# An adjacency-masked two-layer graph kernel: the first mirror's mask moved ahead of strip 4, and half of graph 0's x1 transposed by TensorE

## The chip, the cores and the metric

The kernel runs on one core of a Trainium2 chip. Its time is the device time of one execution in microseconds (us). Engines are named as in the profile: PE is TensorE, DVE is VectorE, ACT is ScalarE, POOL is GpSimd, SP is SyncE, which here only issues transfers (DMAs).

## The reference

There are 16 graphs of 1024 nodes with 256 features each. `adj` holds 0 and 1 and is symmetric. Cut to what matters:

```python
# layer 0
h = x
e0 = leaky(einsum('bid,bjd->bij', h * a0[:, 0], h))    # leaky slope 0.2
alpha = sigmoid(where(adj == 1, e0, -big))
x = layernorm(x + einsum('bij,bjd->bid', alpha, h) + bias)
# layer 1
H = x @ W
s, d = H @ a_src, H @ a_dst
e = where(adj != 0, exp(-leaky_relu(s[:, :, None] + d[:, None, :], 0.2)), 0)
h_prime = einsum('bnm,bmo->bno', e, H) / rowsum(e)
x = layernorm(x + elu(h_prime))
```

The reference has further cases for `adj` values 2 to 4. The kernel has a second, general pass for them, which runs only if a flag says that such values occur; with these inputs it doesn't.

## The kernel before

`one_kind_pass` works through the graphs in one order that is written out by hand: inside it the framework does not reorder, so each engine runs its instructions as the Python code emits them, and waits where an operand or a buffer is not ready. Everything is float32, but for `adj`, which is bfloat16. A graph's 1024 nodes are eight tiles of 128 rows; 256 features are two chunks of 128. "x1" is the output of layer 0.

Each graph b goes through three stages.

*Strips.* The scores are symmetric, so only the upper triangle is computed. `strip(b, jt)` (L194 to L218) makes rows jt*128 onward of the triangle: PE multiplies (`pe`, L208) in chunks of up to 512 columns, ACT takes two hyperbolic tangents of each chunk (L216 into `tb`, L217 into `low`), DVE takes the larger (L218). `tb` has four buffers, `low` two, the PSUM tile `pe` three. `finish` (L220) multiplies by the adjacency into `al` on DVE (L224) and lets POOL add the diagonal (L234). The lower triangle is the mirror of the upper one. For graphs 1 and up it goes through DRAM: `dump(b, t)` turns 32x32 blocks of strip t on DVE (L240) and writes them with four SP transfers (L244), and `gather(b, t)` (L248) reads them back in one SP transfer as column t of the rows below. The gathered values still lack the adjacency; `mask(b, t)` (L252 to L255) multiplies it in on DVE, in one instruction for rows 1 to 3 and one for rows 4 to 7 where t is 0. Column tile 0 of `al` is thus complete only after `mask(b, 0)`.

Beside the strips of graph b, layer 1 of graph b-1 is prepared: `project(b-1, t)` (L354) multiplies tile t of the transposed x1 (`x1T`) by W on PE (`pH`, L368), and three ACT instructions take the result to `H` and `pq` (L376 to L378). The list `projects` says after which strip which tiles are projected. `share_p` (L390) then transposes a column of `pq` on PE (`prow`, L394), copies it on ACT, and sends it through DRAM to all partitions with two POOL transfers (L398, L400).

*sum0.* `sum0(b, t)` multiplies column tile t of `al` with x: eight matmuls on PE over the row tiles (L315; the profile has two records for each matmul). `t` counts up, so the first one needs column tile 0. DVE adds the bias and takes the statistics, POOL computes the norm, and ACT applies it (`scale0`, L304). In the same stage DVE runs masks 3 to 6 and the weights of layer 1 of graph b-1 (L412).

*sum1.* Layer 1's sum for graph b-1 (L419, again on PE), with the elu, the residual and the second norm.

How x1 is transposed: `save_x1(b, g)` (L337) stores half g (four row tiles) of x1 in DRAM with one SP transfer, `fetch_x1(b, g)` (L345) reads it back with eight SP transfers so that 32x32 blocks stand in transposed places, and `turn_x1(b, g)` (L350) turns each block on DVE (L352). For graphs 1 to 14 all this lies in the sum0 and sum1 stages. For graph 0 there is no sum1 stage ahead of graph 1's strips, so its second half is saved, fetched and turned during graph 1's strips, and its tiles 4 to 7 are projected after strip 7.

The start (graph 0) makes its mirror with PE transposes (`mirror`, L257, L263) and its transposed x likewise (`transpose_x`, L182, L189); `ident` is the identity they use, `ps_t` a PSUM pool of two tiles.

Of the kernel before, what the change touches and what calls it, by code (L numbers as in the profile page):

```python
# [9 lines left out]
F32 = mybir.dt.float32  # L10
# [8 lines left out]
P = 128  # L19
HALF = 512  # L20
# [9 lines left out]
def one_kind_pass(  # L30
# [31 lines left out]
    nc = tc.nc  # L62
    B, N, D = x.shape
    NT = N // P
    ND = D // P
    HT = HALF // P
# [10 lines left out]
    ps_t = ctx.enter_context(tc.tile_pool(name="ps_t", bufs=2, space=PSUM))  # L77
# [22 lines left out]
    def adj_rows(b, j0, j1, columns):  # L100

        for g in range(2):
            k0, k1 = max(j0, g * HT), min(j1, (g + 1) * HT)
            if k0 < k1:
                yield slice(k0, k1), adjs[b, g][:, k0 - g * HT : k1 - g * HT, columns]

    def load_blocks(dst, src, n0, n):


        v = src[ds(n0, n), :].rearrange("(nb nn) (c q dd) -> q c nn nb dd", nn=SQ, c=ND, dd=SQ)  # L110
        for c in range(ND):
            for q in range(P // SQ):
                nc.sync.dma_start(
                    dst[ts(q, SQ), c, ds(n0, n)].rearrange("p (nb dd) -> p nb dd", dd=SQ), v[q, c]
                )
# [19 lines left out]
    ident = const.tile([P, P], F32, tag="ident", name="ident")  # L135
# [58 lines left out]
    def strip(b, jt):  # L194


        if jt == 0:
            als[b] = one.tile([P, NT, N], F32, tag="al", name=f"al_{b}")
        width = N - jt * P
        tb = four.tile([P, N], F32, tag="tb", name=f"tb_{b}_{jt}")  # L200
        tbs[b, jt] = tb
        n_chunks = -(-width // HALF)
        per = -(-(width // P) // n_chunks) * P
        for n, o in enumerate(range(0, width, per)):
            w = min(per, width - o)
            pe = ps_e.tile([P, HALF], F32, tag="e", name=f"pe_{b}_{jt}_{n}")
            for c in range(ND):
                nc.tensor.matmul(  # L208
                    pe[:, 0:w],
                    lhsT=xTs[b][:, c, ts(jt, P)],  # L210
                    rhs=xas[b][:, c, ds(jt * P + o, w)],
                    start=(c == 0),
                    stop=(c == ND - 1),
                )
            low = two.tile([P, HALF], F32, tag="low", name=f"low_{b}_{jt}_{n}")
            nc.scalar.activation(tb[:, ds(o, w)], pe[:, 0:w], AF.Tanh, scale=0.5)  # L216
            nc.scalar.activation(low[:, 0:w], pe[:, 0:w], AF.Tanh, scale=0.5 * SLOPE)  # L217
            nc.vector.tensor_tensor(tb[:, ds(o, w)], tb[:, ds(o, w)], low[:, 0:w], ALU.max)  # L218
# [27 lines left out]
    def gather(b, t):  # L246

        nc.sync.dma_start(  # L248
            als[b][:, t + 1 :, ts(t, P)], mirs[b, t].rearrange("(jt p) i -> p jt i", p=P)
        )  # L250

    def mask(b, t):  # L252
        for js, rows in adj_rows(b, t + 1, NT, ts(t, P)):
            v = als[b][:, js, ts(t, P)]
            nc.vector.scalar_tensor_tensor(v, v, 1.0, rows, ALU.add, ALU.mult)  # L255
# [50 lines left out]
    x1s, mv0s, r0s = {}, {}, {}  # L306
# [22 lines left out]
    def scale0(b, t):  # L329
        scale(x1s[b][:, t, :], *r0s[b][t])  # L330


    x1Ts, Hs, pqs, p_bcs, es = {}, {}, {}, {}, {}
# [3 lines left out]
    def save_x1(b, g):  # L337

        if g == 0:
            x1_rows[b] = dram.tile([N, D], F32, tag="x1_rows", name=f"x1_rows_{b}")  # L340
        nc.sync.dma_start(
            x1_rows[b].rearrange("(t p) d -> p t d", p=P)[:, ts(g, HT), :], x1s[b][:, ts(g, HT), :]
        )

    def fetch_x1(b, g):  # L345
        if g == 0:
            x1Ts[b] = one.tile([P, ND, N], F32, tag="x1T", name=f"x1T_{b}")
        load_blocks(x1Ts[b], x1_rows[b], g * HALF, HALF)

    def turn_x1(b, g):  # L350
        v = x1Ts[b][:, :, ts(g, HALF)]
        nc.vector.transpose(v, v)  # L352

    def project(b, t):  # L354

        if t == 0:
            if b < B - 1:
                H = one.tile([P, NT, D + 1], F32, tag="H", name=f"H_{b}")
                Hs[b] = [H[:, m, :] for m in range(NT)]
            else:  # L360
                Hs[b] = []
                for g in range(2):
                    H = two.tile([P, HT, D + 1], F32, tag=f"adj{g}", name=f"H_{b}_{g}")
                    Hs[b] += [H[:, m, :] for m in range(HT)]
            pqs[b] = small.tile([P, NT, 2], F32, tag="pq", name=f"pq_{b}")
        pt = ps_acc.tile([P, D + 2], F32, tag="acc", name=f"pH_{b}_{t}")
        for c in range(ND):
            nc.tensor.matmul(  # L368
                pt,
                lhsT=x1Ts[b][:, c, ts(t, P)],  # L370
                rhs=Wx[:, c, :],
                start=(c == 0),
                stop=(c == ND - 1),
            )
        w = Hs[b][t][:, D : D + 1]
        nc.scalar.activation(w, pt[:, 1:2], AF.Exp, scale=-SLOPE)  # L376
        nc.scalar.activation(pqs[b][:, t, :], pt[:, 0:2], AF.Exp, scale=SLOPE - 1.0)
        nc.scalar.mul(Hs[b][t][:, 0:D], pt[:, 2:], w)  # L378
# [117 lines left out]
    for b in range(1, B):  # L496
        prev, done = b - 1, b - 2
        last = b == B - 1

        projects = [[0, 1], [2], [3], [4, 5], [6], [7], [], []]  # L500
        if prev == 0:

            projects = [[], [0], [1], [2], [3], [], [], [4, 5, 6, 7]]
            turn_x1(0, 0)
        for jt in range(NT):
            strip(b, jt)
            if prev == 0 and jt == 0:
                for t in range(HT, NT):
                    scale0(0, t)
                save_x1(0, 1)  # L510
            finish(b, jt)
            if jt < NT - 1:
                dump(b, jt)
            if prev == 0 and jt == 1:
                fetch_x1(0, 1)
            if prev == 0 and jt == 6:
                turn_x1(0, 1)
            if jt >= 1:
                gather(b, jt - 1)
            for t in projects[jt]:  # L520
                project(prev, t)
            if jt == (6 if prev > 0 else 7):
                share_p(prev)
            if jt >= 5:
                mask(b, jt - 5)
        check_pq(prev)
        if not last:
            load_x(b + 1)
            new_xT(b + 1)
            load_blocks(xTs[b + 1], x[b + 1], 0, N)  # L530

        for t in range(NT):
            if 1 <= t < 5:
                mask(b, t + 2)
            for m in ([], [], [0, 1], [2], [3], [4], [5], [6, 7])[t]:
                weights(prev, m)
            if done >= 0:
                scale1(done, t)
                if t in (3, 7):
                    store(done, t - 3, HT)  # L540
            sum0(b, t)
            if t == 5 and not last:
                load_adj(b + 1, 0)
            if t in (5, 6):
                scale0(b, 2 * t - 10)
                scale0(b, 2 * t - 9)
            if t == 6:
                save_x1(b, 0)
            if t >= NT - CHECKS:
                check_adj(b, t - NT + CHECKS)  # L550
        if not last:
            load_adj(b + 1, 1)


        for t in range(NT):
            acc = acc1(prev, t, ps_acc, "acc")
            for m in range(NT):
                sum1(prev, t, acc, m)
            if last and t == 6:
                turn_x1(b, 1)  # L560
            if last and t == 7:
                weights(b, 0)
            elu(prev, t, acc)
            if last and t == 7:
                weights(b, 1)
            if t >= 1:
                add(prev, t - 1)
            if t == 0:
                fetch_x1(b, 0)
            if t in (1, 2):  # L570
                scale0(b, 2 * t + 2)
                scale0(b, 2 * t + 3)
            if t == 2:
                save_x1(b, 1)
            if t == 4:
                fetch_x1(b, 1)
                turn_x1(b, 0)
            if not last and t in (3, 5):
                turn_x(b + 1, (t - 3) // 2)
            if not last and t == 6:  # L580
                turn_x1(b, 1)
            if last and t in (5, 6):
                for n in range(HT):
                    project(b, (t - 5) * HT + n)
                spread_p(b, t - 5)
        if not last:
            add(prev, NT - 1)
            r1s[prev] = center(mv1s[prev], f"1_{prev}")
# [53 lines left out]
    t = NT - 1  # L642
# [394 lines left out]
```

## Time and profile before

| what | value |
|---|---|
| runs | 1302.4, 1303.8, 1304.43 us; median 1303.8 |
| profiled execution | 1304.77 us, span 1303.0 us, granted PE clock 0.992 |
| PE, sum0 (L315) | 2048 records, 449.3 us busy, 380 ns each |
| PE, sum1 (L419) | 2048 records, 448.9 us busy |
| PE, strips (L208) | 768 records, 267.3 us busy |
| PE, projections (L368) | 512 records, 129.4 us busy |
| DVE, mask (L255) | 150 instructions, 76.5 us busy, 257 to 979 ns |
| gathers (L248) | 105 transfers, 1.7 to 4.7 us from issue to landing |
| first gather of a graph | 448 KB, median 4.1 us to landing |
| x1 store and fetch | 512 KB, 4.3 us; 64 KB each, 2.5 us |

Times are those of one profiled execution. The span is the time from its first to its last instruction; the run's own time has 1.8 us more. A matmul's record lasts about 380 ns though the next starts some 218 ns later: matmuls overlap, so the step between records is what counts. "Idle before" in a row is the time that the engine stood still just ahead of these instructions, with what released it.

### The profile page before, as it was taken

What the parts mean: (1) busy time and instruction counts of PE and PEld (TensorE: products, weight loads), DVE (VectorE), ACT (ScalarE), POOL (GpSimd) and SP (SyncE); (2) the same over time, 40 slices, a digit from 0 to 9 for tenths busy, and PEclk for the clock granted to TensorE, in tenths of its full rate; (3) what the DMA queues carried; (4) which work ended last, traced back from release to release, by engine and by line L of the source; (5) the groups of instructions that cost most, each with busy time, mean ns of one, the idle gap of its engine ahead of it and who ended that gap; (6) DMA issues with size and microseconds to landing.
All of it is one profiled execution on the core that took longest, in us unless ns stands there. A gap on an engine that the chain in (4) does not pass through costs nothing.

```text
span 1303.0 us, 17447 instructions
## 1 busy us (share of the span) xinstructions
PE 1265.0 (97%) x5445; PEld 1022.0 (78%) x5445; DVE 925.4 (71%) x2000; ACT 650.7 (50%) x1459; POOL 295.3 (23%) x606
## 2 busy tenths in 40 slices
PE   7979999999999999999999999999999999999995
PEld 5758788787877878788787887878778787887884
DVE  5665876868868586786868868587785868768664
ACT  4543544645545564545645545564545735446424
POOL 2212121321212222121221212223121221213203
PEclk9989999999999999999999999999999999999998
DMA  9386487694857948487594956948578594876211
GB/s 215 65 180 118 86 189 140 128 202 84 187 112 170 181 95 193 88 188 155 116 203 82 192 120 155 185 95 198 89 175 172 107 194 83 190 139 129 82 17 68
DMA packets 609173, 181.30 MB, mean 139 GB/s; under 512 B 486200, under 2 KB 591664, under 8 KB 609072
## 3 DMA queue, kind: packets, MB, share of 16 engines
q1 hardware_dynamic: 588480, 138.61, 49.0%
q0 software_dynamic: 20592, 41.48, 18.0%
q8 instruction: 46, 0.75, 0.2%
q14 instruction: 55, 0.45, 0.1%
HBM read 152.44 MB, written 61.14 MB: 164 GB/s over the span
## 4 chain that ended last, share of the span: by engine, by line
PE 82%; issue 5%; SPq 4%; DVE 4%; DMA 3%; POOL 1%; ACT 1%; POOLq 0%; DVEq 0%
PE acc L315 34%; PE acc L419 30%; PE pe L208 13%; PE pH L368 4%; SPq L244 3%; DMA mir<-tb 2%; DVE al L224 1%; DVE tb L240 1%; DVE tb L218 1%; ACT tb L216 1%; DVE al L255 1%; POOL r L285 1%; ACT low L217 0%; DMA x<-in_x 0%; SPq L248 0%
## 5 line engine op out<-in xcount | busy, mean ns | idle before, releaser
L315 PE MATMUL acc<-x,al 128*128 128x256 f32 x2048 | 449.3, 380 | 5.3 <-DVE al L255 5.3
L419 PE MATMUL acc<-H,e 128*128 128x257 f32 x2048 | 448.9, 380 | 0.6 <-DVE e L412 0.6
L315 PEld LDWEIGHTS acc<-x,al 128*128 128x128 f32 x2048 | 386.4, 190 | 62.8 <-DVE al L255 10.9
L419 PEld LDWEIGHTS acc<-H,e 128*128 128x128 f32 x2048 | 387.7, 190 | 58.4 <-DVE e L412 1.3
L208 PE MATMUL pe<-xa,xT 128*128 128x384 f32 (+3 forms) x768 | 267.3, 486 | 0.0
L208 PEld LDWEIGHTS pe<-xa,xT 128*128 128x128 f32 x768 | 141.5, 189 | 86.9 <-issue 46.0
L304 ACT ACTIVATE x<-x,mr,r 128x256 f32<-128x256 f32 x128 | 69.2, 592 | 231.6 <-POOL mr L300 199.9
L412 DVE SCALAR_TENSOR_TENSOR e<-p,pq,adj 128x1024 f32<-128x1024 f32 x128 | 159.8, 1270 | 20.8 <-DMA p<-p_row 17.8
L283 POOL TENSOR_SCALAR ve<-mv 128x4 f32<-128x4 f32 (+3 forms) x51 | 17.9, 350 | 676.5 <-DVE mv L277 671.2
L441 ACT ACTIVATE h<-acc,rinv 128x256 f32<-128x256 f32 x127 | 59.7, 470 | 192.7 <-DVE rinv L436 176.5
L216 ACT ACTIVATE tb<-pe 128x512 f32<-128x512 f32 (+1 forms) x192 | 94.3, 491 | 117.2 <-PE pe L208 78.5
L218 DVE TENSOR_TENSOR tb<-tb,low 128x512 f32<-128x512 f32 (+1 forms) x192 | 103.9, 546 | 60.2 <-ACT low L217 48.9
L368 PE MATMUL pH<-Wx,x1T 128*128 128x258 f32 x512 | 129.4, 387 | 8.5 <-issue 8.4
L435 DVE TENSOR_SCALAR rinv<-acc 128x1 f32<-128x1 f32 x128 | 20.1, 157 | 162.2 <-PE acc L419 162.1
L368 PEld LDWEIGHTS pH<-Wx,x1T 128*128 128x128 f32 x512 | 99.1, 194 | 45.5 <-issue 22.9
L121 ACT ACTIVATE junk<-adj,minus 128x2048 bf16<-128x2048 bf16 x64 | 127.3, 1989 | 0.0
L234 POOL TENSOR_TENSOR al<-ident,al 128x128 f32<-128x128 f32 x128 | 68.2, 533 | 241.2 <-DVE al L224 241.0
L224 DVE SCALAR_TENSOR_TENSOR al<-tb,adj 128x512 f32<-128x512 f32 (+7 forms) x132 | 97.5, 738 | 5.0
L323 DVE SCALAR_TENSOR_TENSOR x<-acc,bias_bc 128x256 f32<-128x256 f32 x128 | 54.0, 422 | 61.9 <-PE acc L315 61.9
L217 ACT ACTIVATE low<-pe 128x512 f32<-128x512 f32 (+1 forms) x192 | 93.0, 485 | 0.0
L255 DVE SCALAR_TENSOR_TENSOR al<-al,adj 128x512 f32<-128x512 f32 (+3 forms) x150 | 76.5, 534 | 1.9 <-DMA al<-mir 1.9
L240 DVE STREAM_TRANSPOSE tb<-tb 128x896 f32<-128x896 f32 (+6 forms) x105 | 74.8, 712 | 3.6
(63 smaller groups left out, 903.7 us busy)
## 6 DMA issues: line engine op xcount, KB each, us to landing
adj<-in_adjT POOLq DMA_DIRECT2D x30, 1024.0 KB, 9.2
x_rows<-x SPq DMA_DIRECT2D x32, 512.0 KB, 4.3
x1T<-x_rows SPq DMA_DIRECT2D x256, 64.0 KB, 2.5
x<-in_x SPq DMA_DIRECT2D x15, 1024.0 KB, 5.9
xT<-in_x SPq DMA_DIRECT2D x120, 128.0 KB, 3.4
out<-y SPq DMA_DIRECT2D x30, 512.0 KB, 5.3
p<-p_row POOLq DMA_DIRECT2D x15, 512.0 KB, 4.3
mir<-tb SPq DMA_DIRECT2D x60, 112.0 KB, 2.4
```

The lines of the kernel that those rows point to most:

```text
L121: nc.scalar.activation(junk, rows, AF.Square, bias=minus1, scale=2.0, accum_out=chk[:, b * CHECKS + n : b * CHECKS + n + 1],)
L208: nc.tensor.matmul(pe[:, 0:w], lhsT=xTs[b][:, c, ts(jt, P)], rhs=xas[b][:, c, ds(jt * P + o, w)], start=(c == 0), stop=(c == ND - 1),)
L216: nc.scalar.activation(tb[:, ds(o, w)], pe[:, 0:w], AF.Tanh, scale=0.5)
L217: nc.scalar.activation(low[:, 0:w], pe[:, 0:w], AF.Tanh, scale=0.5 * SLOPE)
L218: nc.vector.tensor_tensor(tb[:, ds(o, w)], tb[:, ds(o, w)], low[:, 0:w], ALU.max)
L224: nc.vector.scalar_tensor_tensor(als[b][:, jt, c0:c1], tbs[b, jt][:, c0 - jt * P : c1 - jt * P], 1.0, adjs[b, jt // HT][:, jt % HT, c0:c1] ...
L240: nc.vector.transpose(tb, tb)
L255: nc.vector.scalar_tensor_tensor(v, v, 1.0, rows, ALU.add, ALU.mult)
L315: nc.tensor.matmul(acc, lhsT=als[b][:, jt, ts(t, P)], rhs=xs[b][:, jt, :], start=(jt == 0), stop=(jt == NT - 1),)
L368: nc.tensor.matmul(pt, lhsT=x1Ts[b][:, c, ts(t, P)], rhs=Wx[:, c, :], start=(c == 0), stop=(c == ND - 1),)
L412: nc.vector.scalar_tensor_tensor(es[b][:, m, :], p_bcs[b], pqs[b][:, m, 1:2], adjs[b, m // HT][:, m % HT, :], ALU.mult, ALU.min)
L419: nc.tensor.matmul(acc, lhsT=es[b][:, m, ts(t, P)], rhs=Hs[b][m], start=(m == 0), stop=(m == NT - 1),)
```

## The change

Two things change, both in `one_kind_pass`. First, `mask(b, 0)` of every graph from 1 on is emitted before `strip(b, 4)`, where it stood after strip 5's other work; masks 1 and 2 stay after strips 6 and 7. Second, for graph 0 alone, `save_x1`, `fetch_x1` and `turn_x1` of the second half go, and a new function `transpose_x1` after strip 2 makes the same half of `x1T` with eight PE transposes into two PSUM tiles and one ACT copy of each. With it, graph 0's projections 4 to 7 move from after strip 7 to after strips 4, 5 and 6, and its `share_p` from after strip 7 to after strip 6, as for the other graphs.

```diff
+    def transpose_x1(b):
+
+        for c in range(ND):
+            pt = ps_t.tile([P, HT, P], F32, tag="t", name=f"px1T_{b}_{c}")
+            for t in range(HT):
+                nc.tensor.transpose(pt[:, t, :], x1s[b][:, HT + t, ts(c, P)], ident)
+            nc.scalar.copy(x1Ts[b][:, c, ts(1, HALF)], pt.rearrange("p t q -> p (t q)"))
...
         projects = [[0, 1], [2], [3], [4, 5], [6], [7], [], []]
         if prev == 0:
 
-            projects = [[], [0], [1], [2], [3], [], [], [4, 5, 6, 7]]
+            projects = [[], [0], [1], [2], [3, 4], [5, 6], [7], []]
             turn_x1(0, 0)
         for jt in range(NT):
+            if jt == 4:
+                mask(b, 0)
             strip(b, jt)
             if prev == 0 and jt == 0:
                 for t in range(HT, NT):
                     scale0(0, t)
-                save_x1(0, 1)
             finish(b, jt)
             if jt < NT - 1:
                 dump(b, jt)
-            if prev == 0 and jt == 1:
-                fetch_x1(0, 1)
-            if prev == 0 and jt == 6:
-                turn_x1(0, 1)
+            if prev == 0 and jt == 2:
+                transpose_x1(0)
             if jt >= 1:
                 gather(b, jt - 1)
             for t in projects[jt]:
                 project(prev, t)
-            if jt == (6 if prev > 0 else 7):
+            if jt == 6:
                 share_p(prev)
-            if jt >= 5:
+            if jt >= 6:
                 mask(b, jt - 5)
```

## The prediction

> **What bounds the kernel now.** I read the page first, for the engine that fills the span, then stretches of equal work side by side, then the chain of waits and the timeline where they differ.
>
> ```profile
> span 1303.0 us, 17447 instructions
> PE 1265.0 (97%) x5445; PEld 1022.0 (78%) x5445; DVE 925.4 (71%) x2000; ACT 650.7 (50%) x1459; POOL 295.3 (23%) x606
> L315 PE MATMUL acc<-x,al 128*128 128x256 f32 x2048 | 449.3, 380 | 5.3 <-DVE al L255 5.3
> ```
>
> TensorE (PE) is the bound: only its idle or slow stretches are to be won. The last row gives one such place: the matmuls of sum0 (L315) wait 5.3 us in all for the mask (L255). The list of waits says 14 times, at most 0.4 us each. Graphs are numbered by b; 14 is graphs 2 to 15. Next the three first strip stages (graphs 1, 2, 3), each from the first strip to where sum0 runs on, by the view of windows:
>
> ```profile
> core 0: us, PE busy (x) PEld busy (x) DVE busy (x) ACT busy (x) POOL busy (x), PEclk, DMA share, GB/s
> 57.30:92.03 34.73, 25.96 (x82) 16.74 (x81) 23.58 (x39) 17.18 (x53) 7.22 (x16) 0.85 0.69 137
> 147.56:171.11 23.55, 23.17 (x85) 15.06 (x83) 19.07 (x34) 16.19 (x49) 7.37 (x14) 1.00 0.54 106
> 226.25:249.79 23.54, 23.17 (x85) 15.06 (x83) 19.07 (x34) 16.19 (x49) 7.37 (x14) 1.00 0.53 102
> ```
>
> Graph 1 needs 11 us more than the others, at a granted clock of 0.85. The chain of waits (start, us, what) shows where:
>
> ```profile
> 74.01 2.61 PE pe L208 x12
> 76.62 8.43 issue
> 85.05 6.55 PE pH L368 x16
> 91.92 0.28 PE prow L394
> 92.19 7.83 PE acc L315 x36
> ```
>
> PE is through with its strips at 76.62, idles 8.43 us, and then runs the last four projections (16 records of pH) at 0.41 us each; in graph 2, eight records take 1.74 us, 0.218 each. So there is a hole and a slow clock after it. The timeline of graph 1 says what the projections waited for:
>
> ```profile
> 64.98 0.38 SPq L341 DMA_DIRECT2D x_rows<-x  x1
> 65.45 6.07 SPq L244 DMA_DIRECT2D mir<-tb  x8
> 71.57 4.31 SPq L113 DMA_DIRECT2D x1T<-x_rows  x8
> 75.98 0.43 SPq L248 DMA_DIRECT2D al<-mir  x1
> 83.75 1.20 DVE L352 STREAM_TRANSPOSE x1T<-x1T 128x1024 f32<-128x1024 f32 x1
> ```
>
> The second half of x1 goes out (64.98), comes back in eight transfers on SP (71.57), and is turned by VectorE (DVE) at 83.75, behind strip 6 in DVE's order. The fetch also holds back the first gather to 75.98. Last, the end of graph 2's strip stage, by the timeline:
>
> ```profile
> 161.85 0.44 SPq L248 DMA_DIRECT2D al<-mir  x1
> 164.43 0.71 DVE L240 STREAM_TRANSPOSE tb<-tb 128x512 f32<-128x512 f32 x1
> 167.00 0.69 DVE L218 TENSOR_TENSOR tb<-tb,low 128x512 f32<-128x512 f32 x1 [1.86 <-DMA mir<-tb]
> 170.13 0.60 PE L315 MATMUL acc<-x,al 128*128 128x256 f32 x2
> 170.50 1.15 DVE L255 SCALAR_TENSOR_TENSOR al<-al,adj 128x384 f32<-128x384 f32 x2
> 171.11 2.21 PE L315 MATMUL acc<-x,al 128*128 128x256 f32 x9 [0.38 <-DVE al L255]
> ```
>
> sum0 starts at 170.13, does its first row tile (two records), and waits for the first piece of mask 0. DVE has that mask only at 170.50, after strip 5, though it sat idle for 1.86 us ahead of strip 4's L218. Was the data there? For L248 in the window 161:163 the trace answers:
>
> ```profile
> DMA to landing us min/median/max: 4.1/4.1/4.1
> ```
>
> So gather 0 lands at 161.85 + 4.1 = 165.95, inside that idle time.
>
> **What the Trainium skill says.** "TensorE: Matmul & The Clock Gate", Part 1: after an idle window of about 3.4 us the array falls to half rate and warms up again under load. The trace agrees: 0.41 against 0.218 us after 8.43 us idle. The same page, Part 4 (PE-mode transpose): a full 128x128 transpose through PSUM takes about 275 ns in context. Here L263's take 272 to 300 ns and seven of them fill 0.93 us, a step of 0.11. "Perfetto Trace Analysis", Tensor Engine Instruction: DVE and ScalarE (ACT) are strict FIFOs, so a mask waiting for its gather holds strip 4 behind it; the trace always shows one DVE order. "DMA: Bandwidth & Descriptors", Anatomy of one DMA: a transfer has some 2 us fixed, mostly the receipt. The store and fetch that go pay that twice; here they land in 4.3 and 2.5 us (medians).
>
> **The change, part by part.**
>
> Graph 1, removed: one store and eight fetches on SP, one turn on DVE (1.2 us), and with them the hole (8.43) and the slow clock: 16 x (0.41 - 0.218) = 3.1. Together 11.5 us of PE time.
>
> Graph 1, added: eight transposes after strip 2, 8 x 0.11 = 0.9 us on PE, all on the path. Their input is scaled by ACT before 65.0; PE gets there at about 67.5, so no wait. Two ACT copies of 128x512 from PSUM at 0.586 each (L388's row by form), with a step of some 0.5 as L216 and L217 have: about 1.0 us on ACT behind strip 2's tanh, from about 68.8. Before, ACT had caught up by 69.7 (first idle 0.39); with the copies it does by 70.7, about where PE brings strip 3's first chunk. PSUM buffers of strips 3 and 4 need ACT's work on chunks three earlier, done by 68.8. So the copies are hidden; uncovered they would cost 1.0 to 1.2.
>
> Graph 1, moved: projections go to steps 4, 5 and 6, the same instructions (per tile four PE records and three short ACT ones). Project 7 now stands just ahead of share_p's transpose, which waits for ACT's pq: before it waited 0.33 there in the same order, at warm clock I take 0.47 (0.38 for the last record, 0.02, 0.24 for ACT, 0.05, less the step of 0.22). share_p moves from step 7 to 6: its two POOL transfers pass POOL's diagonal of strip 7, as in all later graphs, and that diagonal is needed only by the last tile of sum0, over 20 us later. SP's first gather moves from 75.98 to about 71.6, when the dumps are out.
>
> Graph 1's sum: a stage without stall takes 170.13 - 147.56 = 22.57; plus 0.9, plus 0.47, plus 0.15 that strip 2 already waits for ACT (2.74 against 2.59 in the chain) = 24.1. Before: 34.73. Gain 10.6 us, with sum0 at about 81.4.
>
> Is DVE in time there? It is packed from 65.95 on. It ends strip 3 at 74.56; gather 0, issued at 71.6, lands at 75.7. So mask 0 stalls DVE 1.1 us and ends at 76.8; strips 4, 5, 6 take 1.92 + 1.55 + 1.14, and mask 1's first piece 0.39: done at 81.8. sum0's second tile needs it at 81.4 + 3.48 + 0.87 = 85.8. Slack 4 us.
>
> Graphs 2 to 15, mask 0 ahead of strip 4: two DVE instructions, 1.08 us of DVE's time (170.50 to the next start at 171.58), no DMA. Moved past: L218, L224, L240 of strips 4 and 5. Behind the waiting mask stand strip 4's max (which frees a `low` buffer for ACT), its product (then POOL's diagonal), its turn (then SP's dump 4). Start 165.95, end 167.03 against 167.00 when strip 4's data comes: nothing. In graph 3 the gather takes 4.3 us and the same sum gives 0.3 us delay of strips 4 and 5, which nobody waits for: sum0 reads those rows' own parts from its fifth tile on, and ACT needs the `low` buffer only at 170.06. What goes: PE's stall at 171.11. The records step by 0.218 (27.46 us for 126), so the third could start at 170.13 + 0.436 = 170.57; the stall is 0.54. Next late would be mask 1: after strip 6, whose tanh ends at 170.44, it runs from about 171.7, first piece done at 172.1, needed at 170.13 + 4.35 = 174.5. Slack again. Both-sided bound for one graph: 0.38 (the idle that the row shows, from a modelled end) to 0.54; a loss only in the case below. I take 14 x 0.54 = 7.6. Later stages (weights, sum1, turns) take their time from PE and shift with it.
>
> Sum against the profiled execution, 1304.77 us by the clock of the runs (span 1303.0 and 1.8 around it): 1304.8 - 10.6 - 7.6 = 1286.6. The median of the runs, 1303.8, lies 1 us lower: 1285.6. I say 1286.
>
> **Rivals.** (A) Only graph 1 gains, because something else is late for sum0 in graphs 2 to 15 at the same moment: 1303.8 - 10.6 = 1293. For it: DVE is the second engine. Against: the slacks above, and the wait list names only the mask. (B) Graph 1 gains less: ACT's copies bare (1.2), the transposes at the cold step of 0.22 that L189 shows at the start of the run (0.9 more), a stall of about 1 us on a PSUM buffer: 3 us, 1289. For it: ACT and DVE are behind PE in that stage already. (C) Slower: mask 0 does not go by gather 0 alone. The chain of waits puts a later dump ("DMA mir<-tb", ending at 170.52) ahead of the mask. If the mask can start only at W, DVE stops there, and mask 1, 4.61 us of strips behind, comes late too: PE's stall is W - 168.4 (W + 1.08 + 4.61 + 0.39 against 174.48). With W = 170.52 that is 2.1 us in place of 0.54, in 14 graphs and about the same loss in graph 1: +24 - 10.6 = +13, 1317. It decides from W - 168.4 = 0.54 + 10.6/14, W = 169.7, a landing 7.8 us after the issue. Against: the longest landing of any gather is 4.7 us, and in graph 6 the chain reaches the same mask (485.24) through DVE alone at the same distance from PE. (D) The change doesn't do what it says, the wait merely moving to another release in all stages: within 0.2%.
>
> **How the numbers follow.** Forecast 0.76, B 0.11, A 0.08, C 0.04, D 0.01. The forecast's own ends: 5.3 to 7.6 for the 14 graphs, 9.5 to 11.1 for graph 1, and 1 us of scatter: 1284 to 1290. With B inside and part of A's way, 1283.5 to 1291. Faster by over 0.2% (2.6 us, about what a measurement of this kernel can tell) 0.95, same 0.01, slower 0.04.
>
> **What would show it.** Right: no issue gap in graph 1's chain, its stage near 24 us at a clock near 1.0; no L315 wait for L255 in the list; mask 0 some 4 us after its gather's issue; graph to graph 78.14 us in place of 78.68. Wrong: L218 of strip 4 released by L255 over 2 us late, a new PE wait on mask 1 or on `pe` buffers, or pH records still at 0.4 us.

## The result and the profile after

The changed kernel takes 1285.04 us (median of 4 runs, 1284.06 to 1285.33) against 1303.57 us for the kernel before: a ratio of 0.9856, with a 95% interval of 0.9845 to 0.9868. The gain is 18.5 us by the medians. The two profiled executions lie further apart (spans 1303.0 and 1282.3 us, 20.7), because the one of before, 1304.77 us, is slower than its other runs and the one of after, 1284.06 us, the fastest of its own. All times that follow from traces are differences of these two executions.

From the page after: the span, the share of the engines, and the row of sum0's matmuls, whose idle time before them was 5.3 us.

```profile
span 1282.3 us, 17435 instructions
PE 1258.7 (98%) x5453; PEld 1021.8 (80%) x5453; DVE 923.6 (72%) x1999; ACT 651.9 (51%) x1461; POOL 294.5 (23%) x606
L315 PE MATMUL acc<-x,al 128*128 128x256 f32 x2048 | 445.5, 379 | 0.0
```

The list of waits has no matmul of sum0 any more. The new function moved later lines by 7 or 8: projections are now L376, sum1 is L427, the transpose of share_p is L402.

The view of windows (stretch, its length, busy time of each engine, granted clock, DMA share, GB/s) of the kernel after: graph 1's strip stage, graph 2's, and graph 2's sum0.

```profile
56.86:80.80 23.94, 23.62 (x90) 15.62 (x89) 19.74 (x31) 18.26 (x54) 5.78 (x15) 1.00 0.66 126
136.27:158.84 22.57, 22.57 (x82) 14.86 (x81) 18.87 (x33) 15.76 (x48) 6.90 (x13) 1.00 0.52 100
158.84:186.47 27.63, 27.63 (x130) 24.33 (x129) 22.41 (x47) 12.71 (x23) 8.12 (x14) 1.00 0.90 196
```

And graph 2's sum0 in the kernel before, in the same view:

```profile
170.13:198.41 28.28, 27.90 (x131) 24.25 (x130) 23.29 (x48) 12.71 (x23) 7.64 (x14) 1.00 0.89 185
```

Graph 1's strip stage falls from 34.73 to 23.94 us, a gain of 10.79, and its clock is back from 0.85 to 1.00. Each later sum0 falls from 28.28 to 27.63, a gain of 0.64 or 0.65; in graphs 2 to 15 this makes 9.0. In sum0, PE's busy time now equals the length of the stretch. The change is thus worth 19.8 us by the stages. The other 0.9 of the 20.7 us lies ahead of graph 1's strips and behind graph 15's sum0, where the two kernels do the same. It is scatter: in a second trace of the changed kernel graph 1 starts at 57.98 and not at 56.86.

The chain of waits of the kernel after (start, us, what), at graph 1's transposes, at the end of its strips, and at graph 2's sum0:

```profile
64.34 2.58 PE pe L208 x8
66.92 0.87 PE px1T L359 x8
67.79 0.87 PE pH L376 x4
...
79.05 0.89 PE pH L376 x4
79.93 0.02 issue
79.95 0.17 ACT H L384
80.13 0.07 ACT pq L385
80.20 0.04 issue
80.24 0.28 PE prow L402
...
159.01 27.63 PE acc L315 x128
```

Eight transposes take 0.87 us; the projections run at 0.22 us a record; the hole is gone. What is left is the short wait for ACT ahead of share_p's transpose: of the 23.94 us, graph 2's 22.57 and the transposes' 0.87 leave 0.50 for it. In graph 2 all 128 records of sum0 now follow one another, where before the chain broke after two.

The timeline of the kernel after, graph 1 first, then graph 2:

```profile
67.71 1.08 ACT L360 COPY x1T<-px1T 128x512 f32<-128x512 f32 x2
69.99 0.49 ACT L216 ACTIVATE tb<-pe 128x384 f32<-128x384 f32 x1 [0.61 <-PE pe L208]
70.67 0.44 SPq L248 DMA_DIRECT2D al<-mir  x1
74.14 1.16 DVE L255 SCALAR_TENSOR_TENSOR al<-al,adj 128x384 f32<-128x384 f32 x2 [0.56 <-DMA al<-mir]
...
150.56 0.44 SPq L248 DMA_DIRECT2D al<-mir  x1
154.97 1.16 DVE L255 SCALAR_TENSOR_TENSOR al<-al,adj 128x384 f32<-128x384 f32 x2 [1.11 <-DMA al<-mir]
156.04 0.68 DVE L218 TENSOR_TENSOR tb<-tb,low 128x512 f32<-128x512 f32 x1
158.84 6.42 PE L315 MATMUL acc<-x,al 128*128 128x256 f32 x29
```

ACT makes the two copies and still waits 0.61 us for PE at strip 3, so they are hidden. In graph 2 the mask starts 4.4 us after its gather's issue, at once when the data is there, and strip 4's max (L218) comes at 156.04, 0.4 us after ACT has its data ready. Counted from the start of its stage, this max is 0 to 1.5 us later than before in graphs 2 to 15; PE sees none of it.

### The profile page after: what moved, and what is told of

Read it like the earlier page. It is cut to its first block, busy times and chain, and to the rows that moved or that the text cites. A ratio compares the mean times of both kernels' runs of the same rounds, so it can differ in the third digit from the quotient of the medians.

```text
span 1282.3 us, 17435 instructions
## 1 busy us (share of the span) xinstructions
PE 1258.7 (98%) x5453; PEld 1021.8 (80%) x5453; DVE 923.6 (72%) x1999; ACT 651.9 (51%) x1461; POOL 294.5 (23%) x606
## 4 chain that ended last, share of the span: by engine, by line
PE 93%; issue 4%; POOL 1%; DVE 0%; DMA 0%; ACT 0%; SPq 0%; POOLq 0%
PE acc L315 34%; PE acc L427 30%; PE pe L208 19%; PE pH L376 8%; POOL r L285 1%; DMA x<-in_x 0%; PE pxT L189 0%; PE pal L263 0%; POOL ve L283 0%; DVE e L420 0%; PE prow L402 0%; POOL mr L300 0%; POOL n L288 0%; POOL n L289 0%; POOL n L290 0%
## 5 line engine op out<-in xcount | busy, mean ns | idle before, releaser
L427 PE MATMUL acc<-H,e 128*128 128x257 f32 x2048 | 448.8, 380 | 0.6 <-DVE e L420 0.6
L427 PEld LDWEIGHTS acc<-H,e 128*128 128x128 f32 x2048 | 387.7, 189 | 58.5 <-DVE e L420 1.3
L218 DVE TENSOR_TENSOR tb<-tb,low 128x512 f32<-128x512 f32 (+1 forms) x192 | 103.6, 545 | 32.5 <-ACT low L217 32.1
L376 PE MATMUL pH<-Wx,x1T 128*128 128x258 f32 x512 | 126.6, 381 | 0.0
L376 PEld LDWEIGHTS pH<-Wx,x1T 128*128 128x128 f32 x512 | 97.2, 190 | 36.0 <-issue 14.3
L217 ACT ACTIVATE low<-pe 128x512 f32<-128x512 f32 (+1 forms) x192 | 93.0, 485 | 0.0
L255 DVE SCALAR_TENSOR_TENSOR al<-al,adj 128x512 f32<-128x512 f32 (+3 forms) x150 | 76.4, 534 | 20.6 <-DMA al<-mir 20.6
```

The source lines that it names most:

```text
L376: nc.tensor.matmul(pt, lhsT=x1Ts[b][:, c, ts(t, P)], rhs=Wx[:, c, :], start=(c == 0), stop=(c == ND - 1),)
L427: nc.tensor.matmul(acc, lhsT=es[b][:, m, ts(t, P)], rhs=Hs[b][m], start=(m == 0), stop=(m == NT - 1),)
```

## The experiments

The theory: two gains that don't depend on each other, both PE time. In graph 1 it is the hole with the slow clock behind it, in graphs 2 to 15 the wait for mask 0. DVE's own waits cost nothing as long as mask 1 comes in time for sum0's second tile. The rivals are named with each run. All ratios are against the kernel before on the same chip, with 95% intervals; differences to the changed kernel are judged by the traces.

**The mask alone.** The kernel before, with:

```diff
         for jt in range(NT):
+            if jt == 4:
+                mask(b, 0)
             strip(b, jt)
...
-            if jt >= 5:
+            if jt >= 6:
                 mask(b, jt - 5)
```

> The kernel before with the move of mask 0 alone. Theory (two gains that don't depend on each other: PE's wait for mask 0 in graphs 2 to 15, and the hole in graph 1): graphs 2 to 15 lose 0.65 us each, 9.0 in all, as in the changed kernel. In graph 1 the first gather still goes out behind the fetch and lands near 79.8, so the mask holds strips 4 to 6 and the turn of x1 behind it on DVE: the turn starts near 85.5 instead of 83.75, and the hole grows by 1.8. Sum 1303.6 - 9.0 + 1.8 = 1296.4. Rival (the move is worth something only with the rest of DVE's work made lighter; alone the waiting mask costs what it saves): 1302 to 1305.

Measured: 1297.25 us, ratio 0.9949 (0.9935 to 0.9962). In the trace every sum0 of graphs 2 to 15 takes 27.63 us, as in the changed kernel, so the mask's 0.65 us a graph need nothing else. In graph 1 the hole grew, by the chain of waits of this kernel:

```profile
77.76 9.51 issue
87.27 6.78 PE pH L368 x16
```

9.51 against 8.43 us: DVE waited 5.1 us for the late gather, and the turn of x1 stood behind it. I had expected 1.8 more, not 1.1; the direction is the theory's. The sixteen projection records behind the longer hole took longer too, 6.78 against 6.55 us.

**The transposes alone.** The changed kernel with the mask back behind strip 5:

```diff
-            if jt == 4:
-                mask(b, 0)
             strip(b, jt)
...
-            if jt >= 6:
+            if jt >= 5:
                 mask(b, jt - 5)
```

> The changed kernel with mask 0 back behind strip 5. Theory: graph 1's strip stage falls from 34.7 to about 24.6 (23.9 as changed, and 0.65 because PE now meets the wait for mask 0 there too), graphs 2 to 15 keep their wait. 1303.6 - 10.1 = 1293.5. Rival (graph 1 needs the early mask too, since DVE is packed there): stage 26 to 28, 1296 to 1298.

Measured: 1294.33 us, 0.9928 (0.9915 to 0.9942). Graph 1's stage took the same time as in the changed kernel, and its sum0 27.63 us: no wait for mask 0 there, against my expectation. The mask starts 22.1 us after the stage's first matmul and sum0 after 23.9, while in graph 2 of the kernel before it was 22.9 and 22.6. The list of waits has the old wait in the 14 others:

```profile
PE acc L315 <- DVE al L255: 5.2, 14, 0.4
```

So the two gains are separate; the rival that graph 1 needs the early mask has fallen. By the medians the two runs gain 6.6 and 9.5 us, less than 18.5 together, as the early mask alone makes graph 1's hole longer.

**Where the mask may stand.** Two runs move it from strip 4 to strip 5, and to strip 3.

```diff
-            if jt == 4:
+            if jt == 5:
                 mask(b, 0)
```

> The changed kernel with mask 0 ahead of strip 5, so that DVE never waits for the gather and spends 1.08 us between strips 4 and 5. Theory (all that counts is that mask 0 ends before sum0's second row tile): no PE wait, 1285, within 0.15% of the changed kernel. Rival (the mask has to lie in the idle time ahead of strip 4, else strips 5 to 7 and mask 1 come late): 0.4 us a graph back, 1291.

Measured: 1284.91 us, 0.9853 (0.9838 to 0.9868), and every strip and sum0 stage of the trace equal to the changed kernel's to 0.01 us. The idle time ahead of strip 4 isn't needed: what counts is that mask 0 ends before sum0's second row tile.

```diff
-            if jt == 4:
+            if jt == 3:
                 mask(b, 0)
```

> The changed kernel with mask 0 ahead of strip 3, where its gather has not landed. Theory (DVE's slack against PE is several us, since sum0's second tile is the next to need it): DVE waits some 3.3 us for the gather in every graph and all behind it is 4.4 us later than in the kernel before; mask 1's first piece comes within 0.1 us of sum0's need, so PE stalls 0 to 0.3 us a graph: 1285 to 1289.5. Rival (what DVE waits reaches PE, through the low buffers and ACT): 2 to 3.3 us a graph in 15 graphs, 1315 to 1335.

Measured: 1297.83 us, 0.9947 (0.9931 to 0.9962). Neither figure. The timelines of this kernel, DVE, ACT and PE in graph 2:

```profile
154.61 1.16 DVE L255 SCALAR_TENSOR_TENSOR al<-al,adj 128x384 f32<-128x384 f32 x2 [3.12 <-DMA al<-mir]
```

```profile
200.12 0.47 ACT L450 ACTIVATE y<-acc,rinv 128x256 f32<-128x256 f32 x1 [7.37 <-DMA out<-y]
```

```profile
200.65 20.43 PE L427 MATMUL acc<-H,e 128*128 128x257 f32 x80 [3.36 <-ACT y L450]
```

DVE waits 3.1 us for the gather, as expected. In strips and sum0 of the 14 graphs PE loses only 4.6 us in all over the changed kernel, 0.3 a graph, the upper end of the theory's. Only the sum0 part, 1.7 us, is the theory's path: there PE waits at the second tile, for mask 1. In the strips, 2.9 us, it is the rival's path at a small size. PE waits there for ACT, and ACT for a `low` buffer, a wait that the changed kernel's list doesn't have:

```profile
ACT low L217 <- DVE tb L218: 18.4, 15, 2.0
```

But four sum1 stages lost 11.6 us together (6.4 in the one shown). There ACT waited for the store of the previous result to land before it could write into the single `y` buffer, and PE ran out of accumulators. PE's own waits make up only 6.1 of the 11.6 us. Behind the two longest, 3.36 and 2.34 us, the view of windows has the clock at half (0.50):

```profile
199.47:206.29 6.82, 5.64 (x13) 4.53 (x14) 3.02 (x10) 3.99 (x9) 0.00 (x0) 0.50 0.75 145
991.36:994.77 3.41, 3.41 (x10) 2.68 (x9) 2.42 (x9) 2.85 (x7) 0.00 (x0) 0.50 0.92 147
```

The changed kernel has the same ACT wait, up to 4.7 us in 13 graphs, without reaching PE. The next run tests this path.

**The same, with the store early.** The kernel with the mask ahead of strip 3, with all scaling of the previous result and its two stores in the first half of sum0, ahead of an idle stretch of ACT:

```diff
-                scale1(done, t)
-                if t in (3, 7):
-                    store(done, t - 3, HT)
+                if t < HT:
+                    scale1(done, 2 * t)
+                    scale1(done, 2 * t + 1)
+                if t in (1, 3):
+                    store(done, 2 * t - 2, HT)
```

> The kernel with mask 0 ahead of strip 3, and with the previous result's scaling and two stores issued in the first half of the sum0 stage in place of over all of it. In the kernel with mask 0 ahead of strip 3 alone, PE lost 4.5 us in strips and sum0 and 11.6 us in sum1, there in four graphs, waiting for ACT, which waited for the store of y to land. Theory (DVE's lateness reaches sum1 only by ACT's and SP's order, through that late store into a single y buffer): the 11.6 go, 1289.5. Rival (sum1 is late through the weights or the norm itself): 1297.

Measured: 1290.9 us, 0.9902 (0.9887 to 0.9918). Every sum1 is back at 27.84 us, while strips and sum0 still lose. The list of waits of the previous kernel (mask ahead of strip 3) and of this one, in this order:

```profile
ACT y L450 <- DMA out<-y: 46.8, 14, 7.4
```

```profile
ACT y L450 <- DMA out<-y: 2.0, 1, 2.0
```

The late store was the path.

**The slow clock.** The kernel before, with its hole filled and not closed:

```diff
+            if prev == 0 and jt == 7:
+                busy = ps_t.tile([P, HALF], F32, tag="t", name="busy")
+                for _ in range(9):
+                    nc.tensor.matmul(busy, lhsT=xTs[b][:, 0, 0:P], rhs=xas[b][:, 0, 0:HALF], start=True, stop=True)
             for t in projects[jt]:
                 project(prev, t)
```

> The kernel before with nine matmuls of 128x512 (two records of 0.43 us each, 7.7 us in all) put on PE behind strip 7 of graph 1; nothing reads their result. They fill the hole without closing it. Theory (the four projections are slow since PE idled, by its clock): their step falls from 0.41 to 0.22 us, graph 1 gains 3.1 us, 1300.5. Rival (they are slow because their data has just come or ACT holds their buffers): step stays near 0.4, 1303.6.

Measured: 1301.65 us, 0.9986 (0.9980 to 0.9993, 21 runs). Its chain of waits:

```profile
77.41 7.74 PE busy L523 x18
85.15 0.16 issue
85.31 3.74 PE pH L368 x16
```

The same 16 records take 3.74 us in place of 6.55, after useless work. This shows that they were slow because PE had stood still, as the Trainium skill says ("TensorE: Matmul & The Clock Gate", Part 1), and not through their data. In the trace graph 1's stage gains 3.5 us; the runs show 1.7 (0.9 to 2.6). Why only half is not settled, but the clocks suggest a reason: the profiled execution of the kernel before may have had more of the slow clock than most of its runs. In its trace the clock is at half for 10.24 us:

```profile
80.53:90.77 10.24, 5.72 (x13) 4.52 (x14) 5.25 (x11) 2.64 (x12) 0.91 (x2) 0.50 0.88 181
```

In the traces here such stretches in mid-run last 3.41, 6.82, 10.24 and 13.66 us, in steps of 3.41. One step less would be worth 1.7 us of PE time (an estimate: half of 3.41), which is what the runs lack. Of the 41 runs of the kernel before that ran beside the experiments, 36 list a granted clock of 0.993 as the run's mean; the five at 0.992 or 0.991 took 1304.5 us or more. The profiled one, with 0.992 and 1304.77 us, is like these five. As the other runs have no trace, this is not shown.

**The fetch kept on SP.** The changed kernel with the store and the eight fetches still issued, into a buffer that nothing reads:

```diff
+                save_x1(0, 1)
             finish(b, jt)
...
+            if prev == 0 and jt == 1:
+                load_blocks(xTs[0], x1_rows[0], HALF, HALF)
```

> The changed kernel with the store and the eight fetches of graph 0's second half kept on SP, into a tile that nothing reads. Theory: the first gather of graph 1 goes out near 75.5 in place of 70.7 and lands near 79.4, the mask holds DVE until 80.5, strip 4's max frees its low buffer at 81.2, ACT comes late to strip 6 and to project 7 behind it, and PE waits some 2 us at share_p's transpose: stage 25.5 to 26, 1287. Rival (the transfers on SP cost nothing once PE makes its own transpose): 1285.

Measured: 1286.96 us, 0.9872 (0.9857 to 0.9887). Graph 1's stage is 25.2 us against 23.9. Its chain of waits:

```profile
79.04 3.08 DMA mir<-tb
...
82.23 0.38 ACT tb L216
82.61 0.27 ACT low L217
82.89 0.07 ACT H L384
82.95 0.07 ACT pq L385
83.03 0.04 issue
83.07 0.28 PE prow L402
```

The size was about right (25.5 to 26 expected) and the path wrong. It was not the mask that held ACT last: strip 6 writes into the buffer of strip 2's `tb` (there are four), and the dump of strip 2 stood behind the fetch on SP. The expected path ends not far behind it: strip 4's max, late by the mask, frees the `low` buffer at 82.00, and ACT's L217 of strip 6 starts in it at 82.51. Part of the gain in graph 1, 1.2 us here, is thus SP's queue made shorter.

**share_p back behind strip 7**, so that strip 7 covers its wait; the changed kernel with:

```diff
-            if jt == 6:
+            if jt == (6 if prev > 0 else 7):
                 share_p(prev)
```

> The changed kernel with graph 0's share_p back behind strip 7. Theory: of the 0.54 us that PE waits for ACT ahead of share_p's transpose in graph 1, strip 7's 0.45 us of matmuls now cover most; graph 1's strip stage falls from 23.94 to about 23.5 and the time to 1284.6, which only the trace can show. Rival (the wait is set by something else than the projection just ahead): stage unchanged at 23.9.

Measured: 1287.21 us, 0.9886 (0.9864 to 0.9908), of runs at 1284.5, 1285.0, 1289.4 and 1291.7. The chain of waits shows the wait gone:

```profile
79.87 0.87 PE pH L376 x4
80.74 0.45 PE pe L208 x4
81.18 0.16 PE prow L402
81.34 2.87 PE acc L315 x13
```

The stage falls by 0.46 us, as expected, of which sum0 takes 0.06 back (27.69 us); that is too little for the runs to show. The two long runs list a mean granted clock of 0.994, the short ones 0.995 and 0.996, so PE may have stood still in them, as with the mask ahead of strip 3; they have no trace. The scatter called for a repetition, beside the changed kernel and a candidate with three moves: the mask ahead of strip 5, this one, and the early store.

> The same kernel as the one with share_p alone moved back, whose four runs spread over 1284.5 to 1291.7. Theory (PE has a margin of some 6 us in sum1 against the landing of y's store, and only what delays DVE by several us eats it): 1284.6, the spread was chance in one series, so all runs within 1.5 us. Rival (the late store of y reaches PE at random in any kernel that issues it late): again runs 4 to 7 us above the rest.

> The changed kernel as it is, beside the two above. Theory: 1285.0, within 1 us. Rival of the run above: some runs 4 to 7 us higher.

> A candidate: the changed kernel with mask 0 ahead of strip 5 (DVE doesn't wait for its gather), graph 0's share_p behind strip 7, and the previous result's scaling and stores in the first half of sum0. Theory (PE is the bound and only the 0.46 us of share_p's wait is left to win; the other two moves take away waits that PE doesn't feel): 1284.6, every run within 1 us, and no ACT wait for the store of y in the profile. Rival (that wait of ACT, up to 4.7 us in 13 graphs, reaches PE in part of the runs): below the changed kernel by 1 to 3 us in the median and with less scatter.

Measured, in this order: 1285.25 us (0.9861, 0.9844 to 0.9878), 1285.62 us (0.9857, 0.9841 to 0.9874) and 1285.31 us (0.9856, 0.9840 to 0.9872). The highest of the repeated runs was 1287.06, so the spread did not come back at its size; what made it stays open. In the candidate ACT's wait for `y` falls from 29.3 us to:

```profile
ACT y L450 <- DMA out<-y: 3.1, 3, 1.7
```

The time stays: PE did not feel that wait. None of the three beats the changed kernel by more than can be measured.

## Why the prediction was right

*The bound.* PE was the only engine whose time counted. Every gain is a stretch in which PE had stood still or run slowly, and DVE's new waits (20.6 us for gathers, against 1.9 before) cost nothing.

*Graph 1: 10.6 us predicted, 10.79 measured.* The transposes took 0.87 (0.9 predicted). The copies were hidden, with ACT a little earlier than I had it. Mask 0 waited 0.56 us for its gather and not 1.1, as it landed in 3.4 us and not in 4.1. The wait at share_p was taken as 0.47 and is 0.50. What the sum has too much is the 0.15 us for strip 2, which no longer waits for ACT (2.58 us in the chain). The slow clock as its own term is shown by the filled hole: 6.55 against 3.74 us, 2.8 where 3.1 was predicted. The 0.41 us a record is a mean: most of the 16 records step by 0.43, half speed, and the last few by 0.22.

*Graphs 2 to 15: 7.6 us predicted, 9.0 measured.* The mechanism was right and the size of one term off: the stall of 0.54 a graph was 0.65. I took the step of a record from a stretch of 126 that began with the awaited record, so a longer gap just behind it went into the step unseen. By the record starts in the trace of before, the awaited record came 0.758 us after the one ahead of it in graph 2, and the next 0.320 us later, where the others step by 0.216. The 0.104 us that this second gap has too much belong to the wait and went with it. The low end I gave, 0.38, was the page's idle time, which counts up to a modelled end.

*That mask 1 is next and in time* held. *That nobody waits for strips 4 and 5* held at the delays that the change makes, up to 1.5 us and not the 0.3 predicted. With the mask ahead of strip 3, where strip 4's max is 2.3 to 3.3 us late and strip 3's still more, it did not hold: a little was lost through the `low` buffers, and most by a path that the prediction never named, the store of `y`. *That the chain's "DMA mir<-tb" ahead of the mask was no real wait* held as well: the mask starts with its gather's landing, 4.4 us after the issue where rival C needed 7.8, so C had no ground. Rival A fell with the sum0 stages, B with the hidden copies.

*The total*: 1286 against 1285.04, which is closer than the parts, and that is luck. The predicted gain of 18.2 us was 1.6 below the 19.8 of the stages. The prediction then took off 1.0 us because the median of before lies below the profiled execution. The measured median didn't need it: 1304.8 less 19.8 is 1285.0 already. The two misses cancel in part. That the medians' gain, 18.5 us, is smaller than 19.8 would fit a longer slow stretch in the profiled execution of before than in most runs (see the slow clock).

## What to carry to other kernels

Ask of each in-order engine whether work that another engine will wait for has its data before its turn comes, and whether what it would overtake can bear to be later: moving two instructions forward bought 0.65 us fourteen times, before strip 4 as well as before strip 5. A hole on TensorE costs more than its length, both after a long one (the clock) and after a short one (the record that follows). And before making an engine later for an earlier result, follow what it releases through every in-order queue, stores into reused buffers included.

## What the runs showed of the hardware that was not expected

A wait for mask 0 cost PE 0.10 us beyond itself. In all 14 graphs of the kernel before, the awaited record starts 0.75 to 0.76 us after the one ahead of it and the record behind it 0.320 us later, where 0.216 is usual. The trace shows the awaited record starting together with its own weight load (both at 171.11 us in graph 2) and lasting 0.48 us in place of 0.38. With the mask ahead of strip 3, PE's wait for mask 1 is 0.02 us or less in all graphs but one, and the next record still comes 0.31 to 0.32 us later.

Short waits were enough for the slow clock. The prediction quotes an idle window of about 3.4 us; with the mask ahead of strip 3, a wait of 2.34 us (2.72 between record starts) was followed by 3.41 us at half clock, and one of 3.36 us by 6.82. With the holes of 8.43 and 9.51 us the half clock lasted 10.24 and 13.66 us, part of it before PE worked again.

TensorE's transposes did not slow what followed: the four records of pH behind eight of them took 0.87 us, as elsewhere.
